# Layer 0 attention: a ring of seven score banks, runs of nine scores, and GpSimd sums of two key blocks

## The chip, the core and the metric

The kernel runs on one core of a Trainium2 chip. Its engines work side by side, each through its own queue in order: TensorE (PE in the profile, with its weight loads as PEld), VectorE (DVE), ScalarE (ACT), GpSimd (POOL) and SyncE (SP). They wait for each other through semaphores. DMAs are issued from SP's and POOL's queues. The metric is the device time of one execution in microseconds.

## What is computed

The input is x, 2 images of 256 channels and 64 x 64 pixels. Two layers follow, and each adds its result to x. The change is in layer 0, a multi-head self-attention over all pixels of the normalised input:

```python
n = h * w                                            # 4096 pixels
qkv = jnp.einsum('bchw,oc->bohw', x, qkv_w) + qkv_b[None, :, None, None]
qkv = qkv.reshape(b, 3, num_heads, head_dim, n)      # 8 heads of 32
q, k, v = (qkv[:, 0], qkv[:, 1], qkv[:, 2])
scale = 1.0 / math.sqrt(head_dim)
attn_logits = jnp.einsum('bhci,bhcj->bhij', q, k) * scale
attn_weights = jax.nn.softmax(attn_logits, axis=-1)
out = jnp.einsum('bhij,bhcj->bhci', attn_weights, v)
```

Layer 1 (attention over small blocks and between them, and a convolution branch) is left as it is. All data are float32.

## The kernel before

**Units, blocks, groups.** For each image the 8 heads are cut into 16 groups: one head and one half of the queries, 2048, as four units of 512 (`u`). A group runs over 32 blocks of 128 keys (`j`). One unit of one block is a 128 x 512 piece of exponentials, keys on partitions; a block has four units, a group 128, an image 2048, both images 4096.

**The stages of a unit.** PE makes its scores with one matmul of 512 columns into a PSUM bank (L505). ACT takes the exponential into an SBUF place (L511). PE multiplies it by the values (`quarters`, L521): the four units of a block go to four 32-column strips of the array and add up in one bank, `av`, over the 32 blocks; the matmuls of most blocks are cut into two halves of 256 columns, and each matmul shows as two records in the trace. The row sums of the exponentials (the softmax's denominator) are made by adding the blocks up: DVE adds most blocks into `added` (L550, L553, L558, as pairs of units, 1024 columns, or single ones), and the blocks in `SUMMED` are added in memory instead: GpSimd issues a copy for the first of them (L566) and transfers that add into the same buffers, `acc` and `pair`, for the others (L568). When a group is through, DVE adds `acc` and `pair` to its own sums (L748), PE sums over the partitions with a matrix of ones (`sum_rows`), ACT copies `av` and the row sums out (L762, L598), and the division follows through a few small DMAs (`finish`).

**Banks.** [...] One is `av`. The other seven are three tiles, `sa` with three banks, `sb` with two and `sc` with two, and `scores()` fills them in this order: seven units, three exponentials of 3, 2 and 2 units. A tile is filled again when its exponential is through. When a bank is wanted for row sums, the run has six units and the third bank of `sa` is lent.

**Places.** The exponentials stand in a ring of 28 SBUF places (`RING`), 17 of them in one buffer (`es` in the trace) and 11 in another (`v`, since it shares a buffer with the values). The sizes 3, 2, 2 divide both parts evenly, so no exponential is ever cut. A place is written again when PE, DVE and the transfers have read what it held.

**The order.** PE's, ACT's and DVE's instructions stand in the order in which the program text makes them (`manual_schedule`). The loop at the end of `attention0` alternates: one call of `scores()`, then as many steps of value work as `share` allows (a step is half a block), from the units that were there before this call (`have`). At a group's end it breaks off, so that the copy of `av` comes before the next group's values. POOL's queue holds the copies and adding transfers, SP's the loads of keys, values and queries and the small transfers.

Of the kernel before, what the change touches and what calls it, by code (L numbers as in the profile page):

```python
# [17 lines left out]
P = 128  # L18
B, C, H, W = 2, 256, 64, 64
N = H * W  # L20
T = 512
# [4 lines left out]
NH0 = C // HD0  # L26
# [14 lines left out]
def direct_layers(ctx: ExitStack, tc: tile.TileContext, a: dict, out: bass.AP, bad: bass.AP):  # L41
# [3 lines left out]
    nc = tc.nc  # L45
# [11 lines left out]
    psum = {}  # L57
# [53 lines left out]
    for nm, col in (("wk0", V_BK0), ("wq0", V_BQ0)):  # L111
        b0[nm] = const.tile([P, 2], F32, name="b_" + nm)
        for h in range(NH0):
            r = HD0 * (h % 4)
            nc.scalar.dma_start(
                out=b0[nm][r : r + HD0, h // 4 : h // 4 + 1],
                in_=a["vecs"][64 * (h % 2) : 64 * (h % 2) + HD0, col + h // 2 : col + h // 2 + 1],
# [20 lines left out]
    for u in range(4):  # L138
        nc.gpsimd.dma_start(
            out=bv_last[HD0 * u : HD0 * u + HD0, :], in_=a["bv0"][C - HD0 : C].rearrange("(p o) -> p o", o=1)  # L140
# [31 lines left out]
    for u in range(4):  # L172
        r = HD0 * u
        for half in range(2):
            nc.gpsimd.dma_start(
                out=at_query[r + 2 : r + AT, half, :], in_=a["loc"][0:3, (4 * half + u) * T : (4 * half + u + 1) * T]
# [188 lines left out]
    SC0 = 1.0 / math.sqrt(HD0)  # L365
# [8 lines left out]
    NJ = N // P  # L374
# [76 lines left out]

    RING, RING_A = 28, 17

    SUMMED = (3, 7, 11, 15, 18, 22, 26)

    def summed(g):

        return SUMMED if g else SUMMED[1:]

# [4 lines left out]
    def attention0(b, xts, held):  # L464
# [6 lines left out]
        pair = cpool.tile([P, 2, T], F32, tag="col", name=f"acc_{b}")  # L471

        acc = [es[:, RING_A, :], held["acc"][:, 0, :], pair[:, 0, :], pair[:, 1, :]]
        vals2 = held["v"]
        n_units = NH0 * 2 * NJ * 4
        sums, added, copied = {}, {}, {}
        waiting = []
        last = NH0 * 2 - 1

        places = []  # L480
        n_places = 0

        def at_places(first, n):

            while n > 0:
                at = first % RING
                m = min(n, (RING_A if at < RING_A else RING) - at)
                yield m, es[:, at : at + m, :] if at < RING_A else held["es"][:, at - RING_A : at - RING_A + m, :]
                first, n = first + m, n - m

        def scores(spare):

            nonlocal n_places
            bank = None
            for tag, size in (("sa", 3), ("sb", 2), ("sc", 2)):
                first = len(places)
                n = min(size - (spare and size == 3), n_units - first)
                if n <= 0:
                    break
                sc = psum["sc"].tile([P, size, T], F32, tag=tag, name=f"{tag}_{b}_{first}")  # L500
                if spare and size == 3:
                    bank = sc[:, size - 1, :]
                for i in range(n):
                    g, (j, u) = (first + i) // (4 * NJ), divmod((first + i) % (4 * NJ), 4)
                    nc.tensor.matmul(  # L505
                        sc[:, i, :], held["k", g // 2][:, j * P : (j + 1) * P], held["q", g, u // 2][:, u % 2, :],
                        start=True, stop=True,
                    )
                i = 0
                for m, dst in at_places(n_places, n):  # L510
                    nc.scalar.activation(dst, sc[:, i : i + m, :], AF.Exp, scale=SC0)  # L511
                    i += m
                places.extend(range(n_places, n_places + n))
                n_places += size
            return bank

        def quarters(dst, lhs, rhs, start, stop, part=None):

# [4 lines left out]
        def unit(g, j, u):  # L523
            ((_, e),) = at_places(places[(g * NJ + j) * 4 + u], 1)
            return e[:, 0, :]

        def two_units(g, j, w):

            one, two = (places[(g * NJ + j) * 4 + 2 * w + s] for s in range(2))
            if two == one + 1:  # L530
                runs = list(at_places(one, 2))
                if len(runs) == 1:
                    return [(slice(0, 2), runs[0][1])]
            return [(slice(s, s + 1), unit(g, j, 2 * w + s).unsqueeze(1)) for s in range(2)]
# [23 lines left out]
                    nc.vector.tensor_add(dst[:, s, :], dst[:, s, :], src)  # L558

        def add_in_memory(g, j):  # L560
            assert not waiting or j != summed(g)[0]
            runs = [(acc[u].unsqueeze(1), unit(g, j, u).unsqueeze(1)) for u in (0, 1)]
            runs += [(pair[:, s, :], src) for s, src in two_units(g, j, 1)]
            for dst, src in runs:
                if j == summed(g)[0]:
                    nc.gpsimd.dma_start(out=dst, in_=src)  # L566
                else:
                    nc.gpsimd.dma_start(out=dst, in_=src, accum_op=ALU.add)  # L568

        def work_of(g, j):  # L570


            if (g, j) < (last, NJ - 3):
                add_rows(g, j)
            for part in (None,) if j in (0, NJ - 1) else range(2):
                if part == 1:
                    yield
                quarters(
                    sums[g], held["v"][:, (g // 2) % 2, j, :], lambda u: unit(g, j, u), j == 0, j == NJ - 1, part
                )  # L580
# [150 lines left out]
        def steps():  # L731

            for done in range(NH0 * 2 * NJ):
                g, j = divmod(done, NJ)
                if (g, j) == (last, NJ - 3):
                    assert len(places) == n_units
                    held["rows"] = psum["sc"].tile([P, 3, T], F32, tag="sa", name=f"rows_{b}")[:, 2, :]
                    for i in (NJ - 3, NJ - 2, NJ - 1):
                        add_rows(g, i)
                    sum_rows(g, held["rows"])  # L740
                for _ in work_of(g, j):
                    yield done
                if g and j == 0:

                    for w in range(2):
                        dst = added[g - 1][w]
                        for s in range(2) if w == 0 else (slice(0, 2),):
                            nc.vector.tensor_add(dst[:, s, :], dst[:, s, :], acc[s] if w == 0 else pair)  # L748
                    waiting.clear()
                if g and j == 1:  # L750
                    wanted.append(late[0].send)
                if g and j in (9, 17):
                    next(late[0])
                for what in also.get((g, j), ()):
                    what()
                if j == 4 and g % 2 == 0 and g // 2 + 1 < NH0:
                    fetch_head(b, g // 2 + 1, held)
                if j == NJ - 1:
                    waiting.append(g)
                    avs = w4([P, 2, T], f"avs_{b}_{g}")  # L760
                    if g < last:
                        nc.scalar.copy(avs[:, 0, :], sums[g])  # L762
                    copied[g] = avs
                    late[:] = [finish(g)]
                    next(late[0])
                    if g + 2 < NH0 * 2:
                        fetch_queries(b, g + 2, held)
                yield done + 1

        E = mybir.EngineType  # L770
        with tc.manual_schedule(engines={E.PE, E.Activation, E.DVE}):

            per_group = 2 * NJ - 2
            work, begun, taken = steps(), 0, 0
            scores(False)
            final = False
            while not final:
                have = len(places)  # L780
                use = wanted.pop(0) if wanted else None
                bank = scores(use is not None)
                final = have == n_units
                ready = have // 4
                share = have * per_group // (4 * NJ) - 2

                must = sum(place < n_places + 7 - RING for place in places[: 4 * ready : 4])
                if must % NJ == 1:
                    must += 1
                assert must <= ready  # L790
                here = 0
                while begun < ready and (taken < share or begun < must or final or use is not None):
                    if use is not None and here == 2:
                        use(bank)
                        use = None
                        continue
                    here += 1
                    group = begun // NJ
                    begun = next(work)
                    taken += 1  # L800
                    if begun // NJ > group and begun >= must and not final and use is None:
                        break
                if use is not None:
                    use(bank)
            assert next(work, None) is None
            return *finish_last(last), st
# [585 lines left out]
    for b in range(B):  # L1392
        xts = x_first if b == 0 else ahead["xts"]
        w0 = w0_first if b == 0 else ahead["w0"]
        with tc.tile_pool(name=f"ps0_{b}", bufs=8, space=PSUM) as psum["ps"]:
# [7 lines left out]
            held = project0(b, xn, w0)  # L1403
# [571 lines left out]
```

## Time and profile before

| what | us |
|---|---|
| median of 3 runs (lowest, highest) | 3115.34 (3115.27, 3119.38) |
| span of the profiled execution | 3116.4 |
| layer 0's attention, image 0: 125 to 1163 | 1038 |
| layer 0's attention, image 1: 1672 to 2711 | 1039 |
| DVE additions into the row sums, L558, 1596 instructions | 1713.8 busy |
| exponentials, L511, 1770 instructions | 2058.7 busy |
| scores, L505 | 1303.8 busy |
| value products into `av`, L521, 15872 records | 1012.6 busy |
| GpSimd's copies (L566) and adding transfers (L568), 676 in all | one issue takes 0.54 (L566) or 0.85 to 1.04 (L568) |

The profile is one execution. Busy times of a group of instructions are sums of their durations; where instructions overlap in an engine's pipeline, the sum over groups is larger than the engine's own busy time. A row of the timeline gives the start and the length in microseconds of neighbouring instructions of one kind, merged. A row of a window gives each engine's busy time within it.

### The profile page before, as it was taken

The numbers are of one execution on the slowest core, as the hardware profiler recorded it, in microseconds if no ns is written. First come the engines' busy times: TensorE is split into PE (matmuls) and PEld (weight loads), VectorE is DVE, ScalarE is ACT, GpSimd is POOL, SyncE is SP. The second block draws the span as 40 slices with busy tenths as digits, with TensorE's granted clock in tenths as the row PEclk, the third lists the DMA queues.
The fourth block names the chain that finished last, engine by engine and source line by source line (L and its number), as shares of the span: only waits on it lengthen the run. The fifth ranks groups of instructions, "written<-read, shape, count | busy, mean of one in ns | idle before, by whom it ended". The sixth has DMA issues, their size and how long they took to land. (4 is left out here: it accounts for less than half of the span.)

```text
span 3116.4 us, 62659 instructions
## 1 busy us (share of the span) xinstructions
PE 3031.2 (97%) x25129; PEld 1830.6 (59%) x25129; DVE 2467.0 (79%) x3126; ACT 2313.6 (74%) x2436; POOL 836.7 (27%) x923
## 2 busy tenths in 40 slices
PE   6999999999999999999989999999999999999998
PEld 4555555555555556677755555555555555476765
DVE  4599989999899999856556998989989999834543
ACT  2699999999999984622237999999999999734333
POOL 2022222222222231055301222222222222305440
PEclk9999999999999999999999999999999999999999
DMA  7969679797897761230159687796888975700000
GB/s 241 270 132 185 143 150 172 154 178 150 164 181 154 145 133 33 75 134 29 41 193 268 128 176 151 156 176 138 177 162 164 181 153 123 170 4 4 21 14 22
DMA packets 243787, 424.41 MB, mean 136 GB/s; under 512 B 99112, under 2 KB 109916, under 8 KB 241308
## 3 DMA queue, kind: packets, MB, share of 16 engines
q0 software_dynamic: 94992, 238.36, 39.8%
q1 hardware_dynamic: 147580, 181.68, 21.6%
q8 instruction: 199, 3.26, 0.4%
q14 instruction: 104, 0.85, 0.1%
q10 hardware_dynamic: 912, 0.27, 0.0%
HBM read 119.03 MB, written 68.39 MB: 60 GB/s over the span
## 5 line engine op out<-in xcount | busy, mean ns | idle before, releaser
L558 DVE TENSOR_TENSOR e<-e,es 128x1024 f32<-128x1024 f32 (+1 forms) x956 | 1038.6, 1142 | 79.6 <-ACT es L511 77.9
L521 PE MATMUL av<-es,v 128*32 128x256 f32 (+1 forms) x9644 | 746.7, 390 | 0.0
L558 DVE TENSOR_TENSOR e<-e,v 128x1024 f32<-128x1024 f32 (+1 forms) x640 | 675.2, 1107 | 47.7 <-ACT v L511 46.6
L511 ACT ACTIVATE es<-sa 128x1536 f32<-128x1536 f32 (+1 forms) x444 | 635.7, 1432 | 93.1 <-PE sa L505 54.9
L505 PE MATMUL sa<-q,k 128*128 128x512 f32 x1736 | 561.4, 430 | 9.2 <-ACT avs L598 3.5
L521 PE MATMUL av<-v 128*32 128x256 f32 (+1 forms) x6228 | 506.5, 389 | 0.0
L521 PEld LDWEIGHTS av<-es,v 128*32 128x32 f32 x9644 | 316.1, 109 | 299.4 <-issue 160.6
L505 PEld LDWEIGHTS sa<-q,k 128*128 128x128 f32 x1736 | 280.0, 188 | 291.8 <-issue 135.4
L505 PE MATMUL sc<-q,k 128*128 128x512 f32 x1180 | 371.4, 396 | 1.7 <-ACT es L511 0.7
L505 PE MATMUL sb<-q,k 128*128 128x512 f32 x1180 | 371.0, 395 | 1.1 <-ACT es L511 1.1
L521 PEld LDWEIGHTS av<-v 128*32 128x32 f32 x6228 | 216.5, 109 | 178.6 <-issue 81.2
L511 ACT ACTIVATE es<-sc 128x1024 f32<-128x1024 f32 x296 | 306.9, 1037 | 0.0
L511 ACT ACTIVATE v<-sc 128x1024 f32<-128x1024 f32 x294 | 304.9, 1037 | 0.1
L511 ACT ACTIVATE es<-sb 128x1024 f32<-128x1024 f32 x296 | 302.0, 1020 | 3.8 <-DMA acc<-es 3.8
L511 ACT ACTIVATE v<-sb 128x1024 f32<-128x1024 f32 x294 | 300.0, 1020 | 0.0
L505 PEld LDWEIGHTS sb<-q,k 128*128 128x128 f32 x1180 | 221.2, 188 | 55.4 <-ACT es L511 2.9
L505 PEld LDWEIGHTS sc<-q,k 128*128 128x128 f32 x1180 | 210.5, 188 | 71.8 <-ACT es L511 12.1
L511 ACT ACTIVATE v<-sa 128x1536 f32<-128x1536 f32 (+1 forms) x146 | 209.2, 1433 | 35.6 <-PE sa L505 17.0
L948 PE MATMUL mm<-v,wf 128*128 128x256 f32 x1024 | 227.6, 380 | 1.5 <-DVE z L957 1.5
L568 POOL DMA_DIRECT2D es<-es x116 | 98.9, 853 | 475.6 <-ACT es L511 424.3
L948 PEld LDWEIGHTS mm<-v,wf 128*128 128x128 f32 x1024 | 193.3, 190 | 36.8 <-issue 9.9
L938 POOL TENSOR_TENSOR v<-col 128x512 f32<-128x512 f32 x128 | 165.1, 1316 | 179.2 <-ACT rk_sr L1089 39.2
(262 smaller groups left out, 3179.0 us busy)
## 6 DMA issues: line engine op xcount, KB each, us to landing
acc<-es POOLq DMA_DIRECT2D x128, 512.0 KB, 6.2
acc<-v POOLq DMA_DIRECT2D x84, 512.0 KB, 6.4
es<-es POOLq DMA_DIRECT2D x136, 256.0 KB, 4.5
v<-es POOLq DMA_DIRECT2D x132, 256.0 KB, 5.1
k<-wk_halves SPq DMA_DIRECT2D x64, 512.0 KB
q<-wq_halves SPq DMA_DIRECT2D x256, 128.0 KB
v<-v POOLq DMA_DIRECT2D x90, 256.0 KB, 5.4
es<-v POOLq DMA_DIRECT2D x86, 256.0 KB, 3.9
```

The source lines that it names most:

```text
L505: nc.tensor.matmul(sc[:, i, :], held["k", g // 2][:, j * P : (j + 1) * P], held["q", g, u // 2][:, u % 2, :], start=True, stop=True,)
L511: nc.scalar.activation(dst, sc[:, i : i + m, :], AF.Exp, scale=SC0)
L521: nc.tensor.matmul(dst[HD0 * u : HD0 * u + HD0, n], lhs, rhs(u)[:, n], start=start, stop=stop)
L558: nc.vector.tensor_add(dst[:, s, :], dst[:, s, :], src)
L568: nc.gpsimd.dma_start(out=dst, in_=src, accum_op=ALU.add)
L938: (nc.gpsimd.tensor_add if plus else nc.gpsimd.tensor_sub)(dst, rows(one), rows(two))
L948: nc.tensor.matmul(mm[:, m, r, :], wf[:, k, 4 * r + q, m * P : (m + 1) * P], v[r // 2][:, r % 2, k, :], start=k == 0, stop=k == KC - 1,)
```

## The change

`scores()` no longer fills three tiles but one ring of seven banks, unit after unit. One call makes nine units, with exponentials of 1, 1, 3, 2 and 2 units (`PHASE`). `runs_of` cuts an exponential where it would cross the end of the ring of banks or one of the two ends of the ring of places. Scores and exponentials are declared independent of those of other banks, so a score waits for the exponential that last read its bank, and an exponential for the scores of its banks. A bank for row sums is the next of the ring (`spare_bank`), and it is taken after the run of nine.

The loop calls `scores()` once before each stretch of value work and lets that work reach up to seven units behind the last score made (`behind`). It has rules of its own for a group's end (`ending`) and for the last three blocks of an image.

Block 2 joins `SUMMED`. The first two of the summed blocks (2 and 3; 6 and 7 in group 0) are added together by GpSimd with `tensor_add` into `acc` and `pair`, in place of the copy of the first one; the later blocks are added by transfers as before.

```diff
-    SUMMED = (3, 7, 11, 15, 18, 22, 26)
+    SUMMED = (2, 3, 7, 11, 15, 18, 22, 26)
+
+    def paired(g):
+
+        return (2, 3) if g else (6, 7)
 
     def summed(g):
 
-        return SUMMED if g else SUMMED[1:]
+        return SUMMED if g else (6,) + SUMMED[2:]
...
-        def scores(spare):
+        BANKS = 7
+
+        PHASE = (1, 1, 3, 2, 2)
+        recent = {"pe": [], "act": []}
+        ring = psum["sc"].tile([P, BANKS, T], F32, tag="ring", name=f"ring_{b}")
+
+        def spare_bank():
 
             nonlocal n_places
-            bank = None
-            for tag, size in (("sa", 3), ("sb", 2), ("sc", 2)):
...
+            n_places += 1
+            return ring[:, (n_places - 1) % BANKS, :]
+
+        def runs_of(n):
+
+            at = n_places
+            while n > 0:
+                e = at % RING
+                m = min(n, BANKS - at % BANKS, (RING_A if e < RING_A else RING) - e)
+                yield at, m
+                at, n = at + m, n - m
+
+        def scores():
+
+            nonlocal n_places
+            for size in PHASE:
+                for at, m in list(runs_of(min(size, n_units - len(places)))):
+                    banks = set(range(at % BANKS, at % BANKS + m))
+                    sc = ring[:, at % BANKS : at % BANKS + m, :]
+                    for i in range(m):
+                        unit = len(places) + i
+                        g, (j, u) = unit // (4 * NJ), divmod(unit % (4 * NJ), 4)
+                        made = nc.tensor.matmul(
+                            sc[:, i, :], held["k", g // 2][:, j * P : (j + 1) * P], held["q", g, u // 2][:, u % 2, :],
+                            start=True, stop=True,
+                        )
+                        for past, taken_of in recent["act"]:
+                            if at % BANKS + i not in taken_of:
+                                tc.declare_no_dep(made.ins, past.ins, reason="another bank")
+                        recent["pe"] = (recent["pe"] + [(made, at % BANKS + i)])[-21:]
+                    ((_, dst),) = at_places(at, m)
+                    made = nc.scalar.activation(dst, sc, AF.Exp, scale=SC0)
+                    for past, of in recent["pe"]:
+                        if of not in banks:
+                            tc.declare_no_dep(made.ins, past.ins, reason="another bank")
...
         def add_in_memory(g, j):
-            assert not waiting or j != summed(g)[0]
+            first, second = paired(g)
+            assert not waiting or j != first
+            if j == first:
+                return
+            if j == second:
+                for u in (0, 1):
+                    nc.gpsimd.tensor_add(acc[u], unit(g, first, u), unit(g, j, u))
+                one, two = two_units(g, first, 1), two_units(g, j, 1)
+                if len(one) == len(two) == 1:
+                    nc.gpsimd.tensor_add(pair, one[0][1], two[0][1])
+                else:
+                    for s in range(2):
+                        nc.gpsimd.tensor_add(pair[:, s, :], unit(g, first, 2 + s), unit(g, j, 2 + s))
+                return
             runs = [(acc[u].unsqueeze(1), unit(g, j, u).unsqueeze(1)) for u in (0, 1)]
             runs += [(pair[:, s, :], src) for s, src in two_units(g, j, 1)]
             for dst, src in runs:
-                if j == summed(g)[0]:
-                    nc.gpsimd.dma_start(out=dst, in_=src)
-                else:
-                    nc.gpsimd.dma_start(out=dst, in_=src, accum_op=ALU.add)
+                nc.gpsimd.dma_start(out=dst, in_=src, accum_op=ALU.add)
...
+            behind, reach = 7, sum(PHASE) + 1
             work, begun, taken = steps(), 0, 0
-            scores(False)
-            final = False
-            while not final:
-                have = len(places)
+            while begun < NH0 * 2 * NJ:
+                scores()
                 use = wanted.pop(0) if wanted else None
-                bank = scores(use is not None)
-                final = have == n_units
-                ready = have // 4
+                bank = spare_bank() if use is not None else None
+                final = len(places) == n_units
+                have = n_units if final else len(places) - behind
+                ready = max(0, have) // 4
                 share = have * per_group // (4 * NJ) - 2
 
-                must = sum(place < n_places + 7 - RING for place in places[: 4 * ready : 4])
+                must = sum(place < n_places + reach - RING for place in places[: 4 * ready : 4])
...
                 here = 0
-                while begun < ready and (taken < share or begun < must or final or use is not None):
+                while begun < ready:
                     if use is not None and here == 2:
                         use(bank)
                         use = None
                         continue
+                    ending = taken % per_group >= per_group - 2
+                    if not (taken < share or ending or begun < must or final or use is not None):
+                        break
+                    if not final and begun == NH0 * 2 * NJ - 3:
+                        break
                     here += 1
```

More of the change, by code (lines that the diff above doesn't have):

```diff
@@ L489, in at_places @@
                 first, n = first + m, n - m
-        def scores(spare):
-            nonlocal n_places
-            bank = None
-            for tag, size in (("sa", 3), ("sb", 2), ("sc", 2)):
[L496 to L515, printed above, removed]
@@ new lines, in scores @@
+        def scores():
[20 more added lines that the diff above has]
+                            tc.declare_no_dep(made.ins, past.ins, reason="another bank")
+                    recent["act"] = (recent["act"] + [(made, banks)])[-21:]
+                    places.extend(range(at, at + m))
+                    n_places = at + m
@@ L736, in steps @@
                     assert len(places) == n_units
-                    held["rows"] = psum["sc"].tile([P, 3, T], F32, tag="sa", name=f"rows_{b}")[:, 2, :]
+                    held["rows"] = spare_bank()
                     for i in (NJ - 3, NJ - 2, NJ - 1):
```

## The prediction

> **What bounds the kernel now.** I read the table of busy time first, then the busy time of the two attention windows, then single rounds in the timeline, then the waits.
>
> ```profile
> PE 3031.2 (97%) x25129; PEld 1830.6 (59%) x25129; DVE 2467.0 (79%) x3126; ACT 2313.6 (74%) x2436; POOL 836.7 (27%) x923
> ...
> 125.00:1163.00 1038.00, 1033.92 (x10175) 587.86 (x10174) 956.35 (x979) 968.48 (x919) 278.27 (x339) 1.00 0.80 160
> 1672.00:2711.00 1039.00, 1033.87 (x10174) 587.76 (x10166) 956.30 (x979) 967.88 (x918) 274.46 (x339) 1.00 0.79 159
> ```
>
> The change touches layer 0's attention alone: the two windows, 1038 and 1039 us, 2077 of the span's 3116.4. The other 1039 us are taken as fixed. Columns of a window are PE, PEld, DVE, ACT, POOL. PE, ACT and DVE are busy 99.6, 93 and 92%, but a busy PE may be one that waits in its pipeline, so the rounds have to be looked at:
>
> ```profile
> 140.02 0.96 PE L505 MATMUL sa<-q,k 128*128 128x512 f32 x3
> 140.82 0.63 PE L505 MATMUL sb<-q,k 128*128 128x512 f32 x2
> 141.29 0.63 PE L505 MATMUL sc<-q,k 128*128 128x512 f32 x2
> 141.85 1.93 PE L521 MATMUL av<-es,v 128*32 128x256 f32 x32
> 143.71 0.96 PE L505 MATMUL sa<-q,k 128*128 128x512 f32 x3
> ...
> 145.51 1.50 PE L521 MATMUL av<-es,v 128*32 128x256 f32 x24
> 146.94 0.96 PE L505 MATMUL sa<-q,k 128*128 128x512 f32 x3
> ```
>
> Start to start: seven scores last 141.85 - 140.02 = 1.83 us; sb to sc, two scores, 0.47, so 0.233 each; 7 x 0.233 = 1.63 leaves **0.20 us per score run** that no score accounts for. A value run of 32 records lasts 1.86 us, one of 24 lasts 1.43; a record is (1.86 - 1.43) / 8 = 0.054 us, and 24 x 0.054 = 1.29 leaves **0.14 us per value run**. Each switch between the two array shapes costs. The terms add up: 4096 scores x 0.233 = 954, 588 score runs x 0.20 = 118, 15872 records x 0.054 = 857 and 27 for the 512 of double width, 624 value runs x 0.14 = 87, row sums 35: 2078 us, and the windows are 2077. So PE runs at its own pace throughout. ACT's pace, start to start:
>
> ```profile
> 511.30 1.45 ACT L511 ACTIVATE es<-sa 128x1536 f32<-128x1536 f32 x1
> 512.65 1.02 ACT L511 ACTIVATE es<-sb 128x1024 f32<-128x1024 f32 x1
> 513.55 1.04 ACT L511 ACTIVATE es<-sc 128x1024 f32<-128x1024 f32 x1
> 514.45 0.60 ACT L762 COPY avs<-av 128x512 f32<-128x512 f32 x1
> 514.91 1.50 ACT L511 ACTIVATE es<-sa 128x1536 f32<-128x1536 f32 x1
> ```
>
> Three units cost 1.35 us, two 0.90, a copy of one 0.46: about 0.45 a unit and almost nothing an instruction. And the waits, DVE's and PE's between 189 and 1100 us:
>
> ```profile
> DVE e L558 <- ACT es L511: 35.6, 53, 2.2
> DVE e L558 <- ACT v L511: 20.6, 27, 2.7
> ...
> PE sa L505 <- ACT avs L598: 1.7, 6, 0.3
> ```
>
> DVE waits for exponentials, so it is not the bound, and PE hardly waits. The bound is PE with its switches.
>
> [...] in layer 1:
>
> ```profile
> 1493.12 0.42 DVE L973 TENSOR_TENSOR x<-x,z 128x256 f32<-128x256 f32 x1
> 1493.46 1.49 DVE L975 TENSOR_TENSOR x<-x,z 128x256 f32<-128x256 f32 x1
> 1496.27 2.32 DVE L975 TENSOR_TENSOR x<-x,z 128x256 f32<-128x256 f32 x1
> ...
> 1493.11 2.95 POOL L938 TENSOR_TENSOR v<-col 128x512 f32<-128x512 f32 x2 [1.74 <-ACT res_sr L1089]
> 1496.14 2.17 POOL L934 TENSOR_TENSOR col<-xp 128x1152 f32<-128x1152 f32 x1
> ```
>
> An addition of 0.42 us takes 1.49 beside a GpSimd sum of 512 columns (+1.07) and 2.32 beside one of 1152 (+1.90).
>
> **The change, part by part.**
> (1) Runs of nine. Counted in the two built programs, score runs fall from 588 to 454, value runs from 624 to 490; scores (4096), value matmuls and row sums stay. 134 x (0.20 + 0.14) = **-45.6 us** on PE.
> (2) Exponentials. 1770 (556 of three units, 1180 of two, 26 and 8 of the rest) become 2596 (296, 908 and 1392 of three, two, one). At 1.35, 0.90 and 0.46 that is 400 + 817 + 640 = 1857 us against about 1840: +17 on ACT, which with 31 us of copies is then at 1888 of some 2040. One round: nine units cost 2 x 0.46 + 1.35 + 2 x 0.90 = 4.07 on ACT; PE needs 9 x 0.233 + 0.20 = 2.30 for scores and 1.86 (32 records, 238 of the runs) or 2.29 (40 records, 144 runs) for values: 4.16 or 4.59. PE stays the slower.
> (3) The ring. Scores 8 and 9 of a run take the banks of its scores 1 and 2. An exponential follows the start of its last score by at most 0.48 us (sa's third score starts near 510.82, its exponential at 511.30, behind another); I take 0.43. So exponential 1 may run from 0.43 to about 1.04; score 8 starts at 1.73: 0.7 us spare. The last pair's exponential starts when ACT is through the rest, near 3.7, and ends at 4.7, when score 6 of the next run asks at 4.16 + 1.27 = 5.4: again 0.7. So no stall in a regular round. At a group's end one value run has 56 records (3.15 us) and the next 16: the copy of av (0.46) and a short round then push ACT to the edge of that 0.7. I take 0.2 us in each of 30 groups, **+6** (bounds 0 and 0.7 x 30 = 21).
> (4) Start. The first value run stands behind 18 scores instead of 14, which wait for banks: four exponentials' worth, 1.8 us, less the scores' own 0.9, is about 1 and at most 2 a batch: **+3** (0 to 4).
> (5) DVE. It loses 56 additions of 1024 and 16 of 512; 1216 and 683 ns less about 0.08 of overlap make 56 x 1.136 + 16 x 0.60 = -73 us. GpSimd gains 80 sums of 512 columns and 24 of 1024, and loses the 100 plain copies of L566, whose transfers go too. A sum of 512 stops DVE for 1.07; one of 1024 lies between that and 1.90, I take 1.75: 80 x 1.07 + 24 x 1.75 = +128. Net **+55 on DVE**: 1912.65 + 55 = 1968 of about 2044, 96%. DVE's lag: after block 26 of a group it has 5 blocks of additions (2.27 each against 2 us of arrival), the final sums (2.3), block 1, then GpSimd's sums, then blocks 4 to 6: it falls back by about 3 to 4 us before the summed blocks let it catch up. A place in the ring of 28 comes back after 28 x 0.5 = 14 us; a block is complete after 2 and read in 2.3, so about 9 of lag are free. Hidden, with little left over: **+4** (0 to 15 short of rival B).
> GpSimd's queue: behind the three sums stand block 7's transfers, due 8 us later; the sums take 1.3 + 1.3 + 2.1 and up to three DVE additions between, about 8. Those transfers may start late by a fraction, inside the ring's slack. SP's queue keeps its order.
> Sum: -45.6 + 6 + 3 + 4 = **-33 us**. The profiled span becomes 3083; the median of the runs shown, 3115.3, is 1 below the span, so **3082**.
>
> **Rivals.** A, the forecast: PE is shorter by 22 to 52 us (no stall at all, and a switch pair at 0.39 in place of 0.34; or the stalls of (3) to (5) doubled): 3064 to 3094.
> B, DVE at 96% has no room for waits: it waits now for late transfers of the row sums (14 us in the 911-us window) and at both ends of a batch (9), about 45 us in all; 1968 + 45 = 2013 leaves 31 of 2044, and lag and place then hold ACT in some groups by 0.8 us: 25 us back, about 3107. For it: three engines above 93%. Against: half of the waiting on transfers goes by itself when DVE is late.
> C, slower: the lock. If a GpSimd sum costs DVE more than its own time, because the two must hand over six times in a group, DVE becomes the bound. It decides from (2077 - 45 - 1912.65 + 73) / 104 = 1.85 us a sum, against 1.23 in my count. At 2.2: 1912.65 - 73 + 229 + 45 = 2114, 37 above 2077, so 3152. For it: DVE additions of 1.2 us back to back, where layer 1 has gaps. Against: four L1277 operations in a row there pay no more than the sums' own time.
> D, the ring's coupling: PE waits for a bank in most runs (0.25 us in 454 is +114, too much; 0.1 is 45): no change, 3115. Against it the 0.7 us spare of (3).
>
> **How the numbers follow.** A 0.58, B 0.14, C 0.22, D 0.06. About 0.2% (6 us) is what a measurement can tell from no change. Faster: A and half of B, 0.65; same: a share of B and most of D, 0.06; slower: C and the rest, 0.29. The range runs from 3064 (A's lower end) into C, to 3132; C's upper half and little below A stay outside. The likeliest case's own range is 3064 to 3094.
>
> **What would show it.** Right: score runs of nine last 2.30 us, value runs are unchanged, DVE's idle time in a window falls from 82 to some 35 us, GpSimd's sums take 1.3 and about 2 us with DVE additions beside them at 2.3 or more, PE is still at 99%. Wrong: exponentials that wait for DVE (B, C) or scores in the middle of a run that wait for ACT (D), DVE without idle time, an exponential of one unit at 0.52 or more start to start.

## The result, and the profile after

| | median us | lowest to highest | ratio to before, 95% interval |
|---|---|---|---|
| before | 3116.38 | 3115.27 to 3119.38 | |
| after, 4 runs | 3155.68 | 3149.25 to 3159.77 | 1.0125, 1.011 to 1.014 |

The change makes the kernel slower by 39 us, where the forecast had it faster by 33. The profiled execution took 3149.25 us, with a span of 3147.4. That is at the fast end of its runs, so its rows account for some 31 us of the loss and not for all 39.

The table of busy time and the two attention windows, with the columns core time, PE, PEld, DVE, ACT, POOL, then clock, DMA share and GB/s:

```profile
PE 2998.4 (95%) x25129; PEld 1860.8 (59%) x25129; DVE 2479.1 (79%) x3054; ACT 2344.3 (74%) x3262; POOL 1050.5 (33%) x927
...
119.00:1177.00 1058.00, 1021.77 (x10188) 606.21 (x10188) 963.78 (x942) 988.53 (x1337) 385.02 (x341) 1.00 0.75 143
1677.00:2742.00 1065.00, 1025.50 (x10188) 607.89 (x10188) 963.30 (x943) 988.50 (x1334) 379.34 (x341) 0.99 0.74 142
```

The whole loss lies in layer 0's attention. Measured from its first score to the end of its last value product, the attention of an image took 1043.3 and 1043.7 us before and takes 1057.1 and 1064.1 now. (The windows of the kernel before that are shown above begin some 6 us after that first score.) PE has less to do (1022 and 1026 us busy against 1038.6 and 1038.5 before, measured in the same way), as the change intended, but it now stands idle for 36 and 40 us in windows where it had been idle for 5. DVE is not the bound either: its busy time rose by only 7 us a window, and its idle time is 94 and 102 us. All engines wait, so something makes them wait in turn. The stretches that are not idle look as forecast. One regular round in the timeline of the changed kernel (start, length, engine, line, operation):

```profile
209.55 2.34 PE L526 MATMUL ring<-q,k 128*128 128x512 f32 x9
211.82 2.37 PE L547 MATMUL av<-es,v 128*32 128x256 f32 x40
214.12 2.34 PE L526 MATMUL ring<-q,k 128*128 128x512 f32 x9
```

Nine scores take 211.82 - 209.55 = 2.27 us from start to start and a value run of 40 records 2.30: both as worked out, without a gap.

**The first place where time goes: the row sums.** They are the matmuls of `e` with `ones`, which close a group. First the groups of instructions of the changed kernel, with busy time, mean, and then the engine's idle time ahead of them and what ended it:

```profile
L547 PE MATMUL ring<-e,ones 128*32 128x512 f32 (+1 forms) x272 | 34.4, 578 | 48.7 <-ACT es L535 24.9 <-ACT v L535 23.7
```

The same group in the kernel before:

```profile
L521 PE MATMUL sa<-e,ones 128*32 128x512 f32 x240 | 31.2, 592 | 0.0
```

There was no idle time ahead of row sums, and now there are 48.7 us. One of the 30 places, in the timeline of PE after:

```profile
193.72 2.43 PE L526 MATMUL ring<-q,k 128*128 128x512 f32 x9
196.08 1.07 PE L547 MATMUL av<-es,v 128*32 128x256 f32 x16
198.96 1.06 PE L547 MATMUL ring<-e,ones 128*32 128x512 f32 x8 [1.80 <-ACT v L535]
199.84 1.48 PE L547 MATMUL av<-es,v 128*32 128x256 f32 x24
```

A bracket gives the idle time ahead and its releaser. From the start of the 16 value records to the row sums it is 198.96 - 196.08 = 2.88 us. The same pair of rows in the timeline of the kernel before:

```profile
712.74 1.07 PE L521 MATMUL av<-v 128*32 128x256 f32 x16
713.63 1.04 PE L521 MATMUL sa<-e,ones 128*32 128x512 f32 x8
```

There it is 0.89 us. The median over the 30 places is 2.69 after and 0.89 before; 30 x 1.80 = 54 us of PE. The exponential that the row sums wait for is the last one of the run of nine. It does not touch their bank: `spare_bank` gives them the bank that follows the run's last one. It is a dependency that the program carries, since the whole ring is one tile and only scores and exponentials were declared independent of other banks.

**The second place: sums that last 13 us.** GpSimd's timeline in the changed kernel, at the start of a group:

```profile
841.62 13.01 POOL L593 TENSOR_TENSOR es<-v,es 128x512 f32<-128x512 f32 x1 [16.18 <-ACT es L535]
854.60 1.25 POOL L593 TENSOR_TENSOR v<-v,es 128x512 f32<-128x512 f32 x1
855.82 2.35 POOL L596 TENSOR_TENSOR acc<-es 128x1024 f32<-128x1024 f32 x1
```

The first two rows are the same sum of 512 columns, once in 13.01 us and once in 1.25. DVE at the same time:

```profile
842.00 1.21 DVE L784 TENSOR_TENSOR e<-e,acc 128x1024 f32<-128x1024 f32 x1
843.14 2.35 DVE L576 TENSOR_TENSOR e<-v 128x1024 f32<-128x1024 f32 x2
845.41 6.36 DVE L584 TENSOR_TENSOR e<-e,es 128x1024 f32<-128x1024 f32 x6
851.69 1.81 DVE L584 TENSOR_TENSOR e<-e,v 128x512 f32<-128x512 f32 x2
857.37 2.48 DVE L584 TENSOR_TENSOR e<-e,v 128x1024 f32<-128x1024 f32 x2 [3.86 <-ACT v L535]
```

DVE adds without a gap until 851.69 + 1.81 = 853.50, each addition at its undisturbed length (1.21 us for 1024 columns, 0.68 for 512, as ahead of the sum), and the sum ends at 854.63: 1.13 later, hardly less than the 1.25 us that the sum behind it takes. For 12 us it got next to nothing. The short sums behave alike: in 30 of the 32 groups of the changed kernel the first sum is through 1.1 to 1.3 us after the next gap in DVE's work, or after its own start where DVE stood idle already. In the other two, both long, a DVE instruction of another kind came first (shown under e8). And ACT:

```profile
850.20 1.09 ACT L535 ACTIVATE v<-ring 128x512 f32<-128x512 f32 x2 [1.11 <-PE ring L526]
855.88 1.45 ACT L535 ACTIVATE v<-ring 128x1536 f32<-128x1536 f32 x1 [4.60 <-POOL v L593]
858.19 1.94 ACT L535 ACTIVATE es<-ring 128x1024 f32<-128x1024 f32 x2 [0.86 <-POOL acc L596]
```

The next exponential is to be written where the held-up second sum (`v`, L593) still has to read, so ACT stops for 4.60 us. PE's next scores wait for a bank that this exponential has to free, 3.53 us, and DVE waits 3.86 us for its result. PE at that time:

```profile
857.39 1.53 PE L526 MATMUL ring<-q,k 128*128 128x512 f32 x3 [3.53 <-ACT v L535]
```

The stream of additions, which kept GpSimd out, ran dry only because the sum that it kept out held up the exponentials. Four of the 104 sums of the changed kernel last 11.9 to 13.0 us. ACT waits for GpSimd for 4.6 + 3.1 + 0.9 us in the first window and 5.2 + 4.9 in the second, 18.7 in all, where before it did not.

### The profile page after: what moved, and what is told of

It reads as the page before. It is cut to its first block, busy times and chain, and to the rows that moved or that the text cites. A ratio compares the mean times of both kernels' runs of the same rounds, so it can differ in the third digit from the quotient of the medians.

```text
span 3147.4 us, 63848 instructions
## 1 busy us (share of the span) xinstructions
PE 2998.4 (95%) x25129; PEld 1860.8 (59%) x25129; DVE 2479.1 (79%) x3054; ACT 2344.3 (74%) x3262; POOL 1050.5 (33%) x927
## 3 DMA queue, kind: packets, MB, share of 16 engines
q1 hardware_dynamic: 147580, 181.68, 21.3%
## 5 line engine op out<-in xcount | busy, mean ns | idle before, releaser
L535 ACT ACTIVATE es<-ring 128x512 f32<-128x512 f32 (+2 forms) x1572 | 1203.9, 902 | 44.9 <-PE ring L526 31.0
L526 PE MATMUL ring<-q,k 128*128 128x512 f32 x4096 | 1087.8, 408 | 20.6 <-ACT es L535 10.0
L526 PEld LDWEIGHTS ring<-q,k 128*128 128x128 f32 x4096 | 734.0, 188 | 394.9 <-ACT es L535 126.3
L535 ACT ACTIVATE v<-ring 128x512 f32<-128x512 f32 (+2 forms) x1024 | 781.0, 897 | 43.2 <-PE ring L526 27.4
L604 POOL DMA_DIRECT2D acc<-es x118 | 116.3, 986 | 118.3 <-ACT es L535 38.2
L994 ACT COPY z<-mm 128x512 f32<-128x512 f32 x32 | 18.7, 586 | 183.3 <-PE mm L989 183.3
L593 POOL TENSOR_TENSOR es<-v,es 128x512 f32<-128x512 f32 x8 | 39.2, 4896 | 341.9 <-ACT es L535 325.0
L604 POOL DMA_DIRECT2D es<-v x72 | 61.4, 853 | 267.7 <-ACT v L535 253.5
L604 POOL DMA_DIRECT2D v<-es x112 | 115.8, 1034 | 18.0 <-ACT es L535 10.5
L604 POOL DMA_DIRECT2D acc<-v x78 | 76.8, 984 | 76.6 <-ACT es L535 25.5
L593 POOL TENSOR_TENSOR es<-es 128x512 f32<-128x512 f32 x12 | 44.2, 3683 | 157.9 <-ACT es L535 95.2
```

The lines of the kernel that those rows point to most:

```text
L526: made = nc.tensor.matmul(sc[:, i, :], held["k", g // 2][:, j * P : (j + 1) * P], held["q", g, u // 2][:, u % 2, :], start=True, stop=True,)
L535: made = nc.scalar.activation(dst, sc, AF.Exp, scale=SC0)
L593: nc.gpsimd.tensor_add(acc[u], unit(g, first, u), unit(g, j, u))
```

## The experiments

Two theories were open: the row sums' wait, and GpSimd's sums (held up, or slowing DVE). Each part was taken away alone and both together, and the sums were put into the kernel before.

### e1: row sums independent of other banks' exponentials

```diff
+        lent, n_lent = [], [0]
...
-                nc.tensor.matmul(dst[HD0 * u : HD0 * u + HD0, n], lhs, rhs(u)[:, n], start=start, stop=stop)
+                made = nc.tensor.matmul(dst[HD0 * u : HD0 * u + HD0, n], lhs, rhs(u)[:, n], start=start, stop=stop)
+                if lent:
+                    for past, taken_of in recent["act"]:
+                        if lent[-1] not in taken_of:
+                            tc.declare_no_dep(made.ins, past.ins, reason="another bank")
...
             rows = yield
+            lent.append((n_lent[0] - 1) % BANKS)
             sum_rows(g, rows)
+            lent.clear()
```

`n_lent` is the count of banks given out, noted in `spare_bank`.

> The changed kernel, with the row sums' matmuls declared independent of the exponentials of other banks. Theory 1 (the wait for the last exponential of a run of nine costs PE 1.8 us in each of 30 groups, and that time is lost): the stretch from the value run to the row sums falls from 2.7 to 0.9 us, and the kernel gains 40 to 54 us, to about 3105. Theory 2 (GpSimd's sums and their hold on DVE set the pace, the wait of the row sums lies beside it): the stretch is shorter, but the time stays within 10 us of the changed kernel, 3145 to 3160.

Measured: 3155.73 us, 3147.08 to 3160.02, ratio 1.0124 (1.0107 to 1.0141): the same as the changed kernel. But the wait is gone, as the timeline of PE in e1 shows:

```profile
195.28 1.07 PE L549 MATMUL av<-es,v 128*32 128x256 f32 x16
196.17 1.04 PE L549 MATMUL ring<-e,ones 128*32 128x512 f32 x8
197.03 1.48 PE L549 MATMUL av<-es,v 128*32 128x256 f32 x24
```

It is 0.89 us again. So 54 us of waiting were removed and nothing was gained. What took their place is in GpSimd's groups, first in the changed kernel and then in e1:

```profile
L593 POOL TENSOR_TENSOR es<-es 128x512 f32<-128x512 f32 x12 | 44.2, 3683 | 157.9 <-ACT es L535 95.2 <-DVE e L784 40.5 <-DVE e L576 22.2
```

```profile
L599 POOL TENSOR_TENSOR es<-es 128x512 f32<-128x512 f32 x12 | 65.4, 5452 | 158.5 <-ACT es L537 107.8 <-DVE e L792 50.7
```

The same twelve sums take 5.45 us in the mean and no longer 3.68. Seven sums of e1 last 11.4 to 13.1 us, against four, and all 104 take 303.9 us against 269.3. ACT's waits for GpSimd rise from 18.7 to 39.4 us. In the changed kernel, where PE stops at each group's end, DVE keeps up with the exponentials: it waits 1.60 us for one, from 1.1 us after the start of the sum at 318.4 us, and that sum takes 2.25 us. In e1 DVE comes to the same place 3.4 us later against the exponentials, the gap is gone, and the sum takes 13.11. Three of the seven long sums are such places.

A second cost goes with the long sums. Behind each of the seven PE stands idle for 2.3 to 6.0 us, and in this stop or right behind it the trace of e1 begins a stretch of 3.4 to 10.2 us with a granted clock of 0.50, where the means of e1's two attention windows are 0.99 and 0.98, together about 48 us; the changed kernel has three such stretches, 17.1 us. One such stretch as a window of e1, in the columns given above, and the same work of PE ahead of it and in it:

```profile
2551.90:2562.10 10.20, 7.18 (x39) 3.45 (x40) 7.68 (x10) 5.69 (x8) 8.67 (x8) 0.50 0.56 94
...
2547.48 0.82 PE L549 MATMUL av<-v 128*32 128x256 f32 x11
...
2557.36 1.50 PE L549 MATMUL av<-v 128*32 128x256 f32 x11
```

Eleven records that took 0.82 us take 1.50. From first score to last value product, both images together, PE is idle for 58.2 us in e1 against 74.0 in the changed kernel, but busy for 2062.3 against 2047.1 with the same work. So the idle time fell by 16 us and not by 54, and longer matmuls took back 15. No run changes the clock by itself; that the lower clock makes these 15 us is argued from the stretches above.

### e2 and e3: no GpSimd sums

```diff
-    SUMMED = (2, 3, 7, 11, 15, 18, 22, 26)
+    SUMMED = (3, 7, 11, 15, 18, 22, 26)
...
-        return SUMMED if g else (6,) + SUMMED[2:]
+        return SUMMED if g else SUMMED[1:]
```

`add_in_memory` is that of before: a copy of the first block, and transfers that add the others. e2 has this alone and keeps the row sums' wait; e3 has it together with the edit of e1.

> The changed kernel without GpSimd's sums: blocks 3, 7, ... in memory, the first by a copy, as before; the ring and the runs of nine stay, and so does the row sums' wait. Theory 1: only the four sums of 12 to 13 us and what follows them go, 25 to 35 us, to about 3122; still not faster than before. Theory 2: the whole loss goes and the gain of the longer runs appears, 3085 or less.

> Both edits: no GpSimd sums, and row sums that wait only for their own bank. Theory 1: the two losses add up, so 54 + 30 below the changed kernel, 3070 to 3080, faster than both kernels. Theory 2: as without the sums alone. Theory 3 (DVE, which has 73 us of additions more, becomes the bound without GpSimd's help): 3100 or more, exponentials waiting for DVE.

Measured: e2 3132.32 us (3128.99 to 3134.23), ratio 1.0043 (1.0028 to 1.0057). e3 3092.34 us (3087.27 to 3093.26), ratio 0.991 (0.9894 to 0.9927), faster than both kernels. Without sums the row sums' wait is worth 3132.32 - 3092.34 = 40.0 us, and e2 has it in full, by the group of its row sums:

```profile
L543 PE MATMUL ring<-e,ones 128*32 128x512 f32 (+1 forms) x272 | 35.3, 591 | 48.9 <-ACT es L531 24.7 <-ACT v L531 22.3 <-issue 1.8
```

The sums are worth 3155.73 - 3092.34 = 63.4 us where the row sums are free, and 3155.68 - 3132.32 = 23.4 where they wait. The two losses hide each other, and neither theory stands alone. By size theory 1 was too high: e2 gained 23 us where it had 25 to 35, and e3 63 where it had 84. In the profiled executions the attention is 58 us longer in e1 than in e3: PE's idle time makes 37 of them (58.2 against 21.3), its longer busy time 21 (2062.3 against 2041.5).

### e4: the sums alone, in the kernel before

The kernel before with the new `SUMMED`, `paired`, `summed` and `add_in_memory`; banks and runs as before.

> The kernel before with GpSimd's sums of two blocks alone: three score tiles, runs of seven. Theory 1 (the sums cost only where DVE's additions stand back to back and GpSimd does not get its turn): 10 to 35 us slower than before, 3126 to 3150, with single sums of 5 us or more. Theory 2: as slow as the changed kernel or slower, 3155 to 3190. If the sums are hidden altogether: 3110 to 3118.

Measured: 3122.13 us (3114.99 to 3130.76), ratio 1.0014 (1.0005 to 1.0024): 4 us, not 63, and less than the 10 to 35 of theory 1. The waits of DVE in e4 between 189 and 1100 us (total, times, longest):

```profile
DVE e L562 <- ACT es L515: 37.9, 51, 2.6
DVE e L562 <- ACT v L515: 14.6, 24, 2.3
```

In 75 places DVE waits for an exponential, 52.5 us in all, and in such a gap a sum gets in. The total does not tell the kernels apart (54.7 us in 69 places in the changed kernel); where the gaps lie does. In 30 of the 32 groups of e4 a gap comes within 4 us of the start of the first sum, in the changed kernel in 28, in e1 in 25. So the sums' cost is not fixed: it depends on whether DVE's work has a gap when a sum is ready. Two sums of 11.7 and 11.8 us are found here too; behind each ACT waits 2.4 to 2.5 us, and the trace shows no lower granted clock there.

### e5 and e6: a pause in DVE's stream behind each sum

```diff
                 for u in (0, 1):
                     nc.gpsimd.tensor_add(acc[u], unit(g, first, u), unit(g, j, u))
+                    seen = small.tile([P, 1], F32, tag="seen", name=f"seen_{b}_{g}_{u}")
+                    nc.vector.tensor_copy(seen, acc[u][:, :1])
```

DVE copies one column of each of the first two sums and so has to wait for it. e5 is e1 with this, e6 the changed kernel with this. If the sums are kept out by DVE's stream, forcing DVE to wait must make the kernel faster, where the row sums' wait made it slower (40.0 us, e2 against e3).

> The changed kernel with free row sums, and behind each of GpSimd's first two sums a DVE copy of one column of what that sum writes, so that DVE stands still until the sum is through. Theory 1 ([...] it waits for the end of the stream): no sum above 4 us, exponentials wait no longer for GpSimd, and the kernel gains 50 us or more on the same kernel without the pause (3156): 3080 to 3105. Theory 2 (the long sums wait for something else, a transfer or their inputs): the sums stay at 12 to 13 us, DVE stands still for as long, and the time is 3160 or more.

> The changed kernel with the pause alone; the row sums wait as in the changed kernel. Theory 1: about as without the sums and with that wait (3132), 3120 to 3140, and 30 to 45 above the kernel with both. If the row sums' wait is hidden whatever GpSimd does: within 10 us of the one with both edits.

Measured: e5 3096.52 us (3096.33 to 3098.85), ratio 0.9937 (0.992 to 0.9954); e6 3129.18 us (3128.39 to 3134.7), ratio 1.004 (1.0025 to 1.0054). The same sums as at 841.62 above, in GpSimd's timeline of e5:

```profile
831.83 5.01 POOL L599 TENSOR_TENSOR es<-v,es 128x512 f32<-128x512 f32 x1 [15.98 <-ACT es L537]
836.81 1.27 POOL L599 TENSOR_TENSOR v<-v,es 128x512 f32<-128x512 f32 x1
```

DVE in e5:

```profile
833.35 2.35 DVE L582 TENSOR_TENSOR e<-v 128x1024 f32<-128x1024 f32 x2
836.87 0.15 DVE L601 COPY seen<-es 128x1 f32<-128x1 f32 x1 [1.18 <-POOL es L599]
```

DVE's stream now ends at 833.35 + 2.35 = 835.70, and the sum ends at 836.84, again 1.14 after the stream. No sum of e5 or e6 lasts over 5.1 us. That is above the 4 that were expected, since DVE's additions ahead of the pause still keep this sum out for 3.9 us. DVE now waits 74.7 us for sums, in 64 waits, and the kernel is 59 us faster than e1. The table of the six:

| median us | row sums wait for the last exponential | wait for their own bank alone |
|---|---|---|
| GpSimd sums | 3155.68 | 3155.73 (e1) |
| GpSimd sums, DVE pauses | 3129.18 (e6) | 3096.52 (e5) |
| no GpSimd sums | 3132.32 (e2) | 3092.34 (e3) |

With the pause the sums cost 4 us (e5 against e3, with intervals that overlap), and the row sums' wait is worth 32.7. e5 and e6 were measured on another chip than e1, e2 and e3; the kernel before took 3117.22 us there and 3117.81 on the other.

### e8: a gap without a wait

A rival remained: that DVE's wait helped by its order or by delaying DVE, and not by leaving the sum room. e8 is e1 with an instruction on DVE that reads nothing from SBUF and waits for nothing new, ahead of each addition of block 4 (8 in group 0), 64 in all:

```diff
+            if j == (8 if g == 0 else 4):
+                gap = small.tile([P, 1], F32, tag="gap", name=f"gap_{b}_{g}_{j}_{w}")
+                nc.vector.memset(gap, 0.0)
```

> Free row sums and GpSimd's sums, and a DVE memset of one column ahead of each of the two additions of block 4 (block 8 in group 0), 64 in all: an operation without an SBUF input in the stream, that waits for nothing of GpSimd. [...] these openings are enough: no sum above 6 us, 3085 to 3110. If the stream must stop altogether, the memset changes nothing: sums of 12 to 13 us as before it, 3145 to 3165.

Measured: 3103.35 us (3100.84 to 3103.92), ratio 0.9954 (0.9937 to 0.9971). GpSimd in e8:

```profile
831.12 5.01 POOL L602 TENSOR_TENSOR es<-v,es 128x512 f32<-128x512 f32 x1 [15.72 <-DVE e L795]
836.10 2.27 POOL L602 TENSOR_TENSOR v<-v,es 128x512 f32<-128x512 f32 x1
838.33 3.36 POOL L605 TENSOR_TENSOR acc<-es 128x1024 f32<-128x1024 f32 x1
```

DVE in e8:

```profile
834.92 2.30 DVE L593 TENSOR_TENSOR e<-e,es 128x1024 f32<-128x1024 f32 x1
834.94 0.06 DVE L577 MEMSET gap<- 128x1 f32 x1
837.15 2.30 DVE L593 TENSOR_TENSOR e<-e,es 128x1024 f32<-128x1024 f32 x1
...
839.37 3.39 DVE L593 TENSOR_TENSOR e<-e,es 128x1024 f32<-128x1024 f32 x1
```

An operation of 0.06 us between two additions is enough: the sum is through 1.2 us after the memset, and the addition behind it takes 2.30 us, its own 1.2 and the sum's 1.1. From there on the two engines take turns, and the third addition needs no memset for it. The 64 memsets are worth 52 us against e1. In e8 ACT still waits 5.6 us for GpSimd during the attention, in e5 not at all; whether that makes the 7 us between them was not tested.

The changed kernel has such an opening without any edit. Two of its four long sums end where DVE has an instruction with a single SBUF input (`BATCH_NORM_STATS2`) between its additions. GpSimd and DVE in the changed kernel:

```profile
2537.33 11.87 POOL L593 TENSOR_TENSOR es<-es 128x512 f32<-128x512 f32 x1 [16.26 <-DVE e L784]
...
2548.00 0.69 DVE L311 BATCH_NORM_STATS2 stats_l<-x 128x6 f32<-128x512 f32 x1
2548.60 1.69 DVE L584 TENSOR_TENSOR e<-e,es 128x1024 f32<-128x1024 f32 x1
```

The sum is through at 2549.20, 1.2 us after that instruction began, and the addition behind it takes 1.69 us; DVE does not stop in between.

### e7: the order of the exponentials in a run

e3 with the large exponentials first:

```diff
-        PHASE = (1, 1, 3, 2, 2)
+        PHASE = (3, 2, 2, 1, 1)
```

> Free row sums and no GpSimd sums (3092), with exponentials of 3, 2, 2, 1 and 1 units in place of 1, 1, 3, 2 and 2. Scores 8 and 9 of a run then take banks of the first exponential of three, which ends near 1.0 + 1.46 = 2.5 us instead of 1.0 and 1.5, and score 8 starts at 1.7: PE waits 0.8 us in each of 450 runs less what the value runs take up later. If the small exponentials at the front are what lets a run of nine pass seven banks: 100 us slower or more, 3190 to 3450. If the bank wait is hidden: within 15 us of 3092.

Measured: 3370.68 us (3369.66 to 3374.38), ratio 1.0817 (1.0799 to 1.0835), 278 us above e3. PE's timeline in e7:

```profile
507.51 1.91 PE L524 MATMUL ring<-q,k 128*128 128x512 f32 x7
510.08 0.73 PE L524 MATMUL ring<-q,k 128*128 128x512 f32 x2 [0.66 <-ACT v L533]
510.74 2.37 PE L545 MATMUL av<-es,v 128*32 128x256 f32 x40
```

Scores 8 and 9 need the banks of scores 1 and 2, and an exponential of three starts only after score 3: PE stops 0.66 us ahead of the last two scores. The two exponentials of one unit at the front are what keeps the ring free; in the changed kernel these stops are absent from regular rounds.

### e9, e10 and e11: DVE's divisions later

In e3 ACT still waits 10.6 us for adding transfers that are late (5.6 before), and DVE stops for the divisions' small transfers: between 189 and 1100 us, by the waits of e3,

```profile
DVE avs L643 <- DMA avs<-drec: 26.3, 6, 6.7
DVE span L634 <- DMA dense<-dsum: 18.7, 6, 6.6
```

that is 45 us in which its queue stands. If these stops cause the late additions, moving the two steps of a division later in the group should bring time back. The rival is that they fall where DVE has nothing urgent to do.

```diff
-                    if g and j in (9, 17):
+                    if g and j in ((9, 17) if g == last else (14, 24)):
```

e9 is e3 with it, e10 the kernel before with it, e11 is e5 with it.

> Free row sums, no GpSimd sums (3092), and the two steps of a group's division that DVE takes in its queue moved from blocks 9 and 17 of the next group to 14 and 24. DVE stood there for transfers, 45 us in the 911 us between 189 and 1100 (14.5 in the kernel before). Theory: this makes DVE late, late additions hold places, and this is a part of the gain of 46 that did not come (24 came): 5 to 15 us faster, 3077 to 3088. Rival: DVE makes that time up, nothing waits for it: within 4 us of 3092.

> The kernel before with the same two steps moved. Its DVE waits for exponentials 56 us in that stretch and PE for nothing, so it should not matter: 3114 to 3121. If it gains as much as the other, the moved steps have nothing to do with the ring.

> Free row sums, GpSimd's sums with the pause (3096), and the moved steps. If DVE is still the engine that others wait for, GpSimd's help shows at last: below the kernel without the sums. If not: within 8 us of it, 3080 to 3095.

Measured: e9 3088.17 us (3086.72 to 3092.72), ratio 0.9904 (0.989 to 0.9919); e10 3117.44 us (3114.56 to 3123.47), ratio 1.0 (0.9992 to 1.0008); e11 3088.9 us (3085.26 to 3095.3), ratio 0.9906 (0.9893 to 0.9919). e9 cannot be told from e3 (0.991), and e10 is exactly before. There the rival held: where the divisions stand makes no clear difference. e11 against e5 is 0.9906 to 0.9937, and the intervals just miss each other; all five runs of e11 lie below all four of e5, so some 8 us are probably gained there, for a reason that was not traced (they were measured on different chips, where the kernel before took 3118.42 and 3117.22 us). e9, e11 and e3 are the fastest versions, 25 to 30 us below the kernel before, and e3 and e9 do it without GpSimd's sums.

## Why the prediction was wrong, step by step

The sum gave -33 us and the change brought +39. The forecast failed in two steps, and each was a wait that no term of the sum held.

**The failed step of part (5)** is the one on GpSimd's queue: "the sums take 1.3 + 1.3 + 2.1 and up to three DVE additions between, about 8", and the later transfers "may start late by a fraction, inside the ring's slack". It supposed that the two engines hand over after each addition. At the four long sums they did not: the one in the place shown took 13.01 us and was through 1.13 us after DVE's stream of two-input additions had ended, and the two that ended at an instruction of another kind took 11.9. The prediction saw in its rows of layer 1 what a sum costs an addition beside it (1.49 us for 0.42), and priced that on DVE's side alone. In e8 an addition and a sum follow one after the other (2.30 = 1.2 + 1.1). Which of the two comes next was not asked, and the trace shows it: during the four long sums it was DVE again at each addition, until its stream opened; once a sum is under way the two can alternate (e8, sums of 2.27 us beside additions of 2.30). The sums kept out then held places, and exponentials waited for them. The step cost 23 us in the changed kernel and 63 once the row sums were free.

**The failed step of part (1)** is "scores (4096), value matmuls and row sums stay". Their number stayed, and what they wait for did not. Before, the row sums' bank was the third of `sa`; after, it is part of one tile with all exponentials, and the run's last exponential became their condition. A count of instructions shows nothing of this. The wait is worth 40.0 us without sums, 32.7 with paused sums, and nothing visible in the changed kernel itself, since the held-up sums take the gain away (e1).

Without the two, e3 stands at 3092.34 - 3117.81 = -25.5 us against the kernel before, measured along with it. For it the sum's parts (1), (3) and (4) give -45.6 + 6 + 3 = -37. Measured from first score to last value product, PE is busy 2041.5 us in e3 against 2077.0 before, 35.5 less where (1) had 45.6, and idle 21.3 against 10.0, 11 more where (3) and (4) had 9. ACT's waits for late adding transfers, 5 us more than before, are one possible part of the idle time. Of the 10 us that are missing from (1), about 5 is an estimate for the clock: e3 has 13.6 us with a granted clock of 0.50 in its attention, the kernel before 3.4, and about half of the 10.2 us between them is lost if matmuls are as slow there as in the stretch of e1 (1.50 us for 0.82). The rest was not settled.

The other steps:

- Runs of nine: 454 score runs and 490 value runs; the median run of nine lasts 2.28 us for 2.30 and the value run of 40 records 2.30 for 2.29. Right.
- Exponentials: one, two and three units take 0.478, 0.905 and 1.33 us from start to start, for 0.46, 0.90 and 1.35. Right within 0.02 us; 2596 instructions on ACT in place of 1770 are not what holds PE.
- The ring: no stops in regular rounds, and e7 shows that it hangs on the two small exponentials in front. Rival D fell. The start's +3 was not measured by itself.
- DVE: forecast +55 us busy, measured 963.78 + 963.30 against 956.35 + 956.30, so +14. A kept-out sum costs DVE nothing while it waits (additions of 1024 columns take 1.21 us beside the sum of 13.01, as ahead of it), and 29 of the 80 sums of 512 columns take under 1.3 us, as if alone. So the toll was over-sized where it was looked for. Where the two engines do take turns, a sum of 512 columns costs an addition 1.1 us (2.30 for 1.2 in e8; forecast 1.07) and one of 1024 costs 2.2 (forecast 1.75): 3.39 beside 3.36 in e8.
- Rival C said 3152 us, close to the 3155.68 by luck: its cause is wrong. It made DVE the bound, and DVE is idle for 94 us or more a window, where even the forecast had 35.
- "What would show it wrong" named exponentials that wait for DVE and scores in mid-run. They wait for GpSimd, which was not on the list.

## What to carry to other kernels

Where two engines hold each other up, as GpSimd's sums and DVE's additions do here (2.30 us for an addition of 1.2), ask of each what happens if the other never pauses, and look at who waits for the slower one's reads: a sum that is off the critical path holds the places it still has to read. When tiles are merged, check every user of the merged tile for what it now waits for, the rare ones too; their number does not change, only their conditions. When PE is made to stop, look at the granted clock behind the stop too (0.50 for 3.4 to 10.2 us in e1). And remove suspects together as well as one by one: here the two removals alone brought 0 and 23 us, and together 63.

## What the runs showed of the hardware that was not expected

- A GpSimd sum of 512 columns (1.25 to 1.3 us alone) lasted 11.4 to 13.1 us beside an unbroken stream of DVE additions with two SBUF inputs, and in the place shown ended 1.13 us after the stream. One DVE instruction of 0.06 us without an SBUF input let it in (through 1.2 us later, e8), and the longest was then 5.0 us; in the changed kernel one of 0.69 us with a single SBUF input let it in too (1.2 us).
- A GpSimd sum of 1024 columns takes 2.34 to 2.41 us alone; a DVE addition of 1024 beside it takes 3.39.
- In or right behind PE's stops of 2.3 to 6.0 us at the seven long sums of e1 the granted clock fell to 0.50 for 3.4 to 10.2 us, and eleven value records took 1.50 us in place of 0.82; in the changed kernel, behind the sum of 2537.33, they did as well.
- Cutting exponentials finer is nearly free when they read PSUM back to back: 0.478 us for 512 columns, 0.905 for 1024, 1.33 for 1536, so about 0.05 us for each further instruction.
